# Inverse roots of the norms by ScalarE and small GpSimd products in place of GpSimd's power, and one more scan product on GpSimd

## The chip, the cores and the metric

The kernel runs on one core of one Trainium2 chip. Five engines of that core work side by side, each through its own list of instructions in a fixed order: PE (TensorE, matrix products), DVE (VectorE), ACT (ScalarE), POOL (GpSimd) and SP (SyncE, which here issues the transfers). An instruction starts when those before it on its engine have been taken up and the semaphores it waits for have been raised. The metric is the device time of one execution in microseconds (us).

## The reference

The input is 8 images of 64 channels and 128 x 128 pixels. Each goes through a small filter layer and then through a layer of this shape (cut to what matters here):

```python
def layernorm(x, w, b):
    mu = x.mean(-1, keepdims=True)
    var = ((x - mu) ** 2).mean(-1, keepdims=True)
    return (x - mu) * jax.lax.rsqrt(var + EPS) * w + b

def rmsnorm(x, w):
    return x * jax.lax.rsqrt((x * x).mean(-1, keepdims=True) + EPS) * w

def selective_scan(u, dt, A, Bm, Cm, D, z):
    dt = jax.nn.softplus(dt)
    dA = jnp.exp(jnp.einsum('bdl,dn->bldn', dt, A))
    dBu = jnp.einsum('bdl,bnl,bdl->bldn', dt, Bm, u)
    def comb(c1, c2):
        a1, h1 = c1
        a2, h2 = c2
        return (a1 * a2, a2 * h1 + h2)
    _, hs = jax.lax.associative_scan(comb, (dA, dBu), axis=1)
    y = jnp.einsum('bldn,bnl->bdl', hs, Cm) + D[None, :, None] * u
    return y * jax.nn.silu(z)

for i in range(DEPTH):                       # 2 blocks, each scanned forward and backward
    seq = bimamba_block(seq, ...)            # rmsnorm, projections, two selective_scans, residual
seq = rmsnorm(seq, normf_w)
...
xn = ln4d(x, norm2_w, norm2_b)               # and a feed-forward part with a GELU gate
```

Every norm needs the inverse square root of a mean plus EPS = 1e-5, one number per pixel. The scan runs over all 16,384 pixels of an image, for 128 channels with 16 states each.

## The kernel before

**The scan.** An image is cut into 16 chunks of T = 1024 pixels, and the four directions (two blocks, two ways each) make 64 chunks per image and 512 in all. A chunk has 16 steps u = 0 to 15, each a tile of 128 partitions x 1024 (channels times states). For a step, ACT computes the decay w = exp(a dt) into PSUM (`decay`, line 999), DVE runs the recurrence over 1024 pixels (`scan`, lines 1017 and 1019, one for each direction), and the result is multiplied by C (`product`, lines 1038 and 1041); PE then sums it into y (`collect`, line 1057). The other input of the scan, bu, is made by POOL for two steps at a time, a 128x2048 product with three buffers (`drive`, line 991). So a chunk has 8 drives on POOL and 16 scans on DVE.

**Who multiplies by C.** `on_pool(u)` decides it. It was: not for odd u, not for u = 4 and 12, not for a step just after a GELU, and for u = 8 only in chunks beside the front or the feed-forward part. A step on POOL has its scan written to hs, ACT keeps the last column as the state right after the scan, and POOL multiplies hs one step later (line 1038). A step on DVE has its scan written over w, DVE multiplies right after (line 1041), and ACT keeps the state after that (`keep`, line 1031). With this rule 2,832 of 8,192 products are on POOL.

**The norms.** A `Norm` (lines 400 to 421) squares elsewhere, has PE average the squares of 512 pixels into a 128x8 tile in PSUM (`means`), ACT add EPS and bring it to SBUF (`means_out`, line 411), POOL raise it to the power -0.5 (`root`, line 414), and PE spread the root over the channels (`spread`, line 420), for DVE to multiply with. There are 768: per image 16 x 3 in the front (the two norms that come before the scans, and the first block's), 16 in the mix stage, and 16 in each of the two second directions, where a block's result is normed for what follows.

**The order of the work.** Everything in the main part is put down with a time and a phase, `at(time, phase, fn)`; the list sorted by these two is the order in which the instructions of each engine stand, and nothing reorders them. Time is counted in scan steps; the phases of one step are FEED, SCAN, MID, PROD, DECAY, REST. Chunk i starts at 16 i, its drive k stands at 2k - 5, its products on POOL in FEED one step after their scan, its decay u two steps before its scan. Around the scans run other parts: the front of the next image (a piece every 24 steps, beside the second block), and of the image before the mix stage (every 13 steps, beside the first 12 chunks) and then the feed-forward part with its GELUs (every 24 steps, beside the rest of the first block and a little of the second). The core lines of a norm in a second direction:

```python
at(b + 12, FEED, lambda: n.means(mm_tile, self.sq))
at(b + 13, DECAY, n.means_out)
at(b + 14, REST, n.root)
at(b + 17, FEED, n.spread, mm_tile)
at(b + 18, DECAY, self.normed)
```

**Function tables.** ACT's Silu (line 895), Softplus (line 923), Gelu (line 763) and Exp (line 999) each need another table. The compiler puts a load ahead of the first instruction that needs another one than the one in place. Before, that is once ahead of each Silu, Softplus and Gelu group, and once ahead of the first decay after it.

Of the kernel before, what the change touches and what calls it, by code (L numbers as in the profile page):

```python
# [8 lines left out]
F32 = mybir.dt.float32  # L9
BF16 = mybir.dt.bfloat16  # L10
AF = mybir.ActivationFunctionType
ALU = mybir.AluOpType
# [3 lines left out]
P = 128  # L16
# [3 lines left out]
ROWS = 4  # L20
# [13 lines left out]
G = 4  # L34
U = G * G
PW = W + 2
FEED, SCAN, MID, PROD, DECAY, REST = range(6)

IMAGE = 4 * NT * U
# [16 lines left out]
def kernel(ctx: ExitStack, tc: tile.TileContext, a: dict, out: bass.AP):  # L56
# [6 lines left out]
    nc = tc.nc  # L63
# [8 lines left out]
    def const(shape, name, dt=F32):  # L72
        return wp.tile(shape, dt, tag=name, name=name)
# [3 lines left out]
    def dram(shape, name):  # L77
        return dramp.tile(shape, F32, tag=name, name=name + "_dram")


    def image(name):

        return dram([C, PW * PW + PW], name)

    def pixels(img):
        return img[:, 0 : PW * PW].rearrange("c (r w) -> c r w", w=PW)

    def clear(img):
        nc.sync.dma_start(
            img.rearrange("c (r w) -> c r w", w=PW),  # L90
            zero.rearrange("c (o w) -> c o w", o=1).to_broadcast([C, PW + 1, PW]),
        )

    x_img, xm_img, xn_img = image("x"), image("xm"), image("xn")
    dw_img = [image(f"dw{i}") for i in range(2)]
    zero = const([C, PW], "zero")
    nc.vector.memset(zero, 0.0)
# [11 lines left out]
    nc.vector.tensor_tensor(center, center, ident, ALU.add)  # L109
    eps = const([P, 1], "eps")  # L110
    nc.vector.memset(eps, EPS)
    neg_half = const([P, 2 * ROWS], "neg_half")
    nc.vector.memset(neg_half, -0.5)

    sel_y = const([P, 32, 1], "sel_y")
    nc.vector.tensor_reduce(sel_y, ident.rearrange("k (m n) -> k m n", n=G), AX.X, ALU.add)
# [44 lines left out]
    for h in range(2):  # L161
        nc.sync.dma_start(b1[h * 32 : (h + 1) * 32, :], row(a["L0_conv_b1"]))
        nc.sync.dma_start(w2v[64:65, 9 * h : 9 * h + 9], a["L0_conv_b2"].rearrange("(o k) -> o k", o=1))


    FRONT_W, MIX_W, FFN_W = 9 * 64 + P, 18 * P, 18 * P + 2 * C
    w_dram = [dram([P, n], f"w{i}") for i, n in enumerate((FRONT_W, MIX_W, FFN_W))]
# [190 lines left out]
    wk = ctx.enter_context(tc.tile_pool(name="wk", bufs=2))  # L358
# [19 lines left out]
    def tmp(name):  # L378
        return wk.tile([P, N], F32, tag="tmp", name=name, bufs=14)

    def window(img, name):

        return inp.tile([P, ROWS + 2, PW], F32, tag="win", name=name)

# [14 lines left out]
    class Norm:  # L399
# [7 lines left out]
                )  # L407

        def means_out(self):
            self.r = wk.tile([P, 2 * ROWS], F32, tag="r", name="r", bufs=4)  # L410
            nc.scalar.activation(self.r, self.mp[:, 0 : 2 * ROWS], AF.Identity, bias=eps)  # L411

        def root(self):
            nc.gpsimd.tensor_tensor(self.r, self.r, neg_half, ALU.pow)  # L414

        def spread(self, ps):
            self.rb = ps("rb")
# [15 lines left out]
    class Front:  # L433
        def __init__(self, b, c):
            self.b, self.c, self.p = b, c, b % 2
            self.n1, self.n2, self.n3 = Norm(), Norm(), Norm()
            self.t = {}
# [267 lines left out]
    class Ffn:  # L705
# [55 lines left out]
        def gelus(self):  # L761
            self.gt = tmp("gt")
            nc.scalar.activation(self.gt, self.rest[0], AF.Gelu)
            for h in range(2):
                nc.scalar.activation(self.ga[h], self.ga[h], AF.Gelu)

        def rest_times(self):
            nc.vector.tensor_tensor(self.gt, self.gt, self.rest[1], ALU.mult)
# [29 lines left out]
        def plan(self, a):  # L798
            early = 12 if self.alone else 0
            at(a - 4 - early, REST, self.load, 0)  # L800
            at(a - 3 - early, REST, self.load, 1)

            if self.alone:
                groups = ((0, 0, self.first_out, 2), (3, 2, None, 0), (6, 1, self.times, 9))
                gelus, out = 5, 12
            else:
                groups = ((0, 0, self.first_out, 5), (6, 2, None, 0), (14, 1, self.times, 19))
                gelus, out = GELU, 19
            for t, g, end, to in groups:
                for i in range(4):  # L810
                    at(a + t + (0 if self.alone else i), REST, self.conv, g, i)
                for h in range(2 if end else 0):
                    at(a + to, DECAY, end, h)
            at(a + gelus, REST, self.gelus)
            at(a + gelus + 1, DECAY, self.rest_times)
            at(a + out - 5, REST, self.load_x2)
            at(a + out, REST, self.project)
            at(a + out + 2, DECAY, self.add)
            at(a + out + 2, REST, self.store)

    def plan_ffn(b, a, step):
        at(a - 4, REST, load_weights, 2)
        for c in range(NCH):
            Ffn(b, c).plan(a + step * c)


    gelu_times = {IMAGE * b + FFN_AT + FFN_STEP * c + GELU for b in range(B - 1) for c in range(NCH)}
# [7 lines left out]
    class Chunk:  # L835


        def __init__(self, i):
            self.b, self.l, self.d, self.t, self.second = order[i]
            self.i, self.t0 = i, U * i  # L840
            self.first = i % NT == 0
            self.pairs = PAIRS[i % 2]
            r, last = self.t0 % IMAGE, self.b == B - 1
            self.beside_front = (
                FRONT_AT - FRONT_STEP <= r < FRONT_AT + NCH * FRONT_STEP + 16 and not last
            ) or self.t0 < FIRST_FRONT_AT + NCH * FRONT_STEP + 16
            self.beside_gelu = any(self.t0 - U <= t < self.t0 + 2 * U for t in gelu_times)
            self.prev = None
            self.bus, self.hss, self.ws = {}, {}, {}
            self.dup, self.dtp, self.bp, self.cp, self.yv = {}, {}, {}, {}, {}  # L850
            self.norm = Norm()
# [42 lines left out]
        def silu(self):  # L894
            nc.scalar.activation(self.xc, self.xc, AF.Silu)
            if self.second:
                nc.scalar.activation(self.gt, self.gt, AF.Silu)

        def store_gate(self):
            self.gt_d = sd.tile([DI, T], F32, tag="gate", name="gate_dram", bufs=4)  # L900
            nc.sync.dma_start(self.gt_d, self.gt)
            self.gt = {}
# [18 lines left out]
        def softplus(self):  # L921
            dt = self.dt
            nc.scalar.activation(dt, dt, AF.Softplus)

        def bc(self):
            self.bcp = mm_tile("bcp")
            for i, s in enumerate(halves):
                nc.tensor.matmul(
                    self.bcp[32 * i : 32 * i + 32, :], wbc[:, self.l, self.d, :], self.xc[:, s],
                    start=True, stop=True,  # L930
                )
# [45 lines left out]
        def on_pool(self, u):  # L977


            if u % 2 or u % 8 == 4 or self.t0 + u - 1 in gelu_times:  # L980
                return False
            return u != 8 or self.beside_front or self.beside_gelu

        def over_pair(self, what, k):
# [206 lines left out]
    for b in range(B):  # L1191
# [2 lines left out]
        plan_mix(b, a + (LAST_MIX_AT if last else MIX_AT), LAST_MIX_STEP if last else MIX_STEP)  # L1194
        plan_ffn(b, a + (LAST_FFN_AT if last else FFN_AT), LAST_FFN_STEP if last else FFN_STEP)
    with tc.manual_schedule():
        for key in sorted(steps):
            for fn, args in steps[key]:
                fn(*args)
# [29 lines left out]
```

## Time and profile before

The kernel's time is 30010.1 us (median of 3 runs, 30005.71 to 30014.66). The execution that was profiled took 29956.31 us and its span, from the first to the last instruction, is 29954.4 us.

| | busy us | share of the span | instructions |
|---|---|---|---|
| POOL | 27661.8 | 92% | 8732 |
| DVE | 27086.6 | 90% | 17258 |
| PE | 24257.7 | 81% | 96344 |
| ACT | 18533.8 | 62% | 28316 |

The scans run from about 580 us to 29337 us of the span; before them the weights are made ready and the first front runs, after them the last mix and feed-forward pieces. In a line of the profile, "L1038 POOL TENSOR_TENSOR hs<-hs,cp" is an instruction of line 1038 on POOL that writes the tile hs from hs and cp; then come shapes and count, the busy time in us and the mean duration of one in ns, and behind the last bar the idle time of that engine just before these instructions, with what ended it. A line of waits says who waited for whom, in us in total, how many times, and the longest.

### The profile page before, as it was taken

What the parts mean: (1) busy time and instruction counts of PE and PEld (TensorE: products, weight loads), DVE (VectorE), ACT (ScalarE), POOL (GpSimd) and SP (SyncE); (2) the same over time, 40 slices, a digit from 0 to 9 for tenths busy, and PEclk for the clock granted to TensorE, in tenths of its full rate; (3) what the DMA queues carried; (4) which work ended last, traced back from release to release, by engine and by line L of the source; (5) the groups of instructions that cost most, each with busy time, mean ns of one, the idle gap of its engine ahead of it and who ended that gap; (6) DMA issues with size and microseconds to landing.
All of it is one profiled execution on the core that took longest, in us unless ns stands there. A gap on an engine that the chain in (4) does not pass through costs nothing. (4 is left out here: it accounts for less than half of the span.)

```text
span 29954.4 us, 307972 instructions
## 1 busy us (share of the span) xinstructions
PE 24257.7 (81%) x96344; PEld 8093.1 (27%) x96344; DVE 27086.6 (90%) x17258; ACT 18533.8 (62%) x28316; POOL 27661.8 (92%) x8732
## 2 busy tenths in 40 slices
PE   7666888878888788887888788887888878888579
PEld 3211232223322233222322223222232223322123
DVE  3899999999999999999999999999999999999992
ACT  2566666666666666666666666666666666666661
POOL 3999999999999999999999999999999999999991
PEclk8777888988989888988899889898898988889789
DMA  4776676766777677776777767776677766777672
GB/s 100 210 241 214 221 235 230 237 213 223 237 231 237 213 225 237 232 232 210 233 232 238 225 214 232 232 237 223 215 236 232 240 214 222 235 234 234 214 240 75
DMA packets 2529698, 6617.29 MB, mean 221 GB/s; under 512 B 417862, under 2 KB 722262, under 8 KB 2525750
## 3 DMA queue, kind: packets, MB, share of 16 engines
q1 hardware_dynamic: 2528054, 6597.59, 68.4%
q8 instruction: 761, 12.47, 0.2%
q14 instruction: 883, 7.23, 0.1%
HBM read 5363.40 MB, written 1266.10 MB: 221 GB/s over the span
## 5 line engine op out<-in xcount | busy, mean ns | idle before, releaser
L991 POOL TENSOR_TENSOR bu<-dup,bp 128x2048 f32<-128x2048 f32 x4096 | 18578.8, 4539 | 557.7 <-DVE w L1019 421.4
L999 ACT ACTIVATE w<-dtp,a_neg 128x1024 f32<-128x1024 f32 x8192 | 9162.3, 1118 | 510.2 <-DVE hs L1017 313.9
L1038 POOL TENSOR_TENSOR hs<-hs,cp 128x1024 f32<-128x1024 f32 x2832 | 6685.3, 2361 | 197.9 <-ACT state L1031 133.3
L1041 DVE TENSOR_TENSOR hs<-w,cp 128x1024 f32<-128x1024 f32 x5360 | 6564.9, 1225 | 310.9 <-DMA cp<-bc_dram 77.6
L1017 DVE TENSOR_TENSOR_SCAN w<-w,state,bu 128x1024 f32<-128x1024 f32 x2677 | 6280.9, 2346 | 346.5 <-ACT w L999 345.9
L1019 DVE TENSOR_TENSOR_SCAN w<-w,state,bu 128x1024 f32<-128x1024 f32 x2683 | 6291.0, 2345 | 314.1 <-ACT w L999 313.5
L1057 PE MATMUL y<-hs,sel_y 128*32 128x512 f32 x32768 | 5183.3, 702 | 33.0 <-POOL hs L1038 32.6
L1031 ACT COPY state<-w 128x1 f32<-128x1 f32 x5360 | 837.4, 156 | 5040.0 <-DVE hs L1041 5004.5
L1017 DVE TENSOR_TENSOR_SCAN hs<-w,state,bu 128x1024 f32<-128x1024 f32 x1419 | 3321.3, 2341 | 86.4 <-ACT w L999 36.9
L1019 DVE TENSOR_TENSOR_SCAN hs<-w,state,bu 128x1024 f32<-128x1024 f32 x1413 | 3307.7, 2341 | 52.8 <-ACT w L999 34.7
L1050 PE MATMUL y<-xc,dskip 128*64 128x512 f32 x4096 | 1622.3, 860 | 2025.6 <-ACT yv L1074 1339.3
L869 PE MATMUL xp<-hn,wx 128*128 128x512 f32 x4096 | 2269.2, 682 | 485.3 <-ACT xc L875 339.8
L746 PE MATMUL fp<-fw,bgw 128*128 128x512 f32 (+1 forms) x6144 | 2353.9, 638 | 64.7 <-ACT ga L759 63.5
L1057 PEld LDWEIGHTS y<-hs,sel_y 128*32 128x32 f32 x32768 | 736.8, 116 | 3496.6 <-issue 2469.7
L1031 ACT COPY state<-hs 128x1 f32<-128x1 f32 x2832 | 540.2, 191 | 1829.2 <-DVE hs L1019 929.6
L414 POOL TENSOR_TENSOR r<-r,neg_half 128x8 f32<-128x8 f32 x768 | 1263.5, 1645 | 380.5 <-ACT r L411 323.9
L875 ACT ACTIVATE xc<-xp,cbias 128x512 f32<-128x512 f32 x1024 | 697.2, 681 | 1415.1 <-PE xp L869 1414.7
L910 PE MATMUL dp<-xc,wdt 128*128 128x512 f32 x2048 | 1228.5, 684 | 351.8 <-ACT dt L917 268.2
L752 PE MATMUL fp<-fw,bgw 64*128 64x512 f32 (+1 forms) x6144 | 1501.1, 608 | 0.0
L999 ACT ACT_TABLE_LOAD x1134 | 1454.9, 1283 | 20.1
L947 POOL TENSOR_TENSOR dt<-dt,xc 128x1024 f32<-128x1024 f32 x512 | 1212.8, 2369 | 246.5 <-DMA dt_dram<-dt 223.8
L510 PE MATMUL acc<-t,ident 128*128 128x512 f32 x2304 | 1361.3, 675 | 0.0
(184 smaller groups left out, 26903.7 us busy)
## 6 DMA issues: line engine op xcount, KB each, us to landing
bp<-bc_dram SPq DMA_DIRECT2D x4096, 256.0 KB, 4.0
dup<-du_dram SPq DMA_DIRECT2D x4096, 256.0 KB, 5.0
dtp<-dt_dram SPq DMA_DIRECT2D x4096, 256.0 KB, 5.0
cp<-bc_dram SPq DMA_DIRECT2D x4096, 256.0 KB, 5.0
hn<-hn_dram SPq DMA_DIRECT2D x1024, 256.5 KB, 4.8
dt_dram<-dt SPq DMA_DIRECT2D x512, 512.0 KB, 3.1
du_dram<-dt SPq DMA_DIRECT2D x512, 512.0 KB, 2.6
yf_dram<-yv SPq DMA_DIRECT2D x512, 256.0 KB, 4.4
```

What stands on the lines that cost most here:

```text
L746: nc.tensor.matmul(o, wpair[:, i, g, m], self.win[h][:, i : i + ROWS, 0:W], start=(i == 0), stop=False)
L752: nc.tensor.matmul(o, wlast[rows, i, g, m], self.win[h][rows, i : i + ROWS, lo : W + lo], start=False, stop=(i == 2),)
L869: nc.tensor.matmul(self.xp[h], wx[:, self.l, self.d, i, :], self.hn2[:, s.start + 2 * i : s.stop + 2 * i], start=(i == 0), stop=(i == 1),)
L991: nc.gpsimd.tensor_tensor(bu, self.dup[self.pairs[k][1]], self.over_pair("bp", k), ALU.mult)
L999: nc.scalar.activation(w, self.dtp[gp][:, i, :], AF.Exp, scale=a_neg[:, self.l, self.d, g, j : j + 1])
L1017: nc.vector.tensor_tensor_scan(to, w, bu, s0, ALU.mult, ALU.add)
L1019: nc.vector.tensor_tensor_scan(to[:, ::-1], w[:, ::-1], bu[:, ::-1], s0, ALU.mult, ALU.add)
L1031: nc.scalar.copy(self.column(u), h[:, T - 1 : T] if self.d == 0 else h[:, 0:1])
L1038: nc.gpsimd.tensor_tensor(hs, hs, c, ALU.mult)
L1041: nc.vector.tensor_tensor(hs, w, c, ALU.mult)
L1050: nc.tensor.matmul(self.y[C * h : C * h + C, :], dskip[:, self.l, self.d, C * gp : C * gp + C], self.xc[:, s], start=True, stop=False,)
L1057: nc.tensor.matmul(self.y[lo : lo + 32, :], sel_y, hs[:, i, s], start=False, stop=(k % 4 == 3))
```

## The change

In a norm, ACT now does four small activations on the 128x8 tile instead of one: r = ln(mean + EPS), v = mean + EPS, r = exp(-0.5 r), q = r squared. POOL does three small instructions instead of the power: q = q v, q = -0.5 q + 1.5, r = r q, which is one Newton step on the root. A function table that holds both Exp and Ln is asked for by name once at the start and right after each Silu, Softplus and Gelu group (the last image's GELUs excepted).

The second part is `on_pool`: step u = 4 is now on POOL in the chunks of a second direction beside the front, and in those chunks beside the feed-forward part whose steps 0 and 8 do not come just after a GELU. That is 175 of the 512 chunks (105 and 70), so 3,007 products are on POOL and 5,185 on DVE.

```diff
@@ -109,8 +111,6 @@
     eps = const([P, 1], "eps")
     nc.vector.memset(eps, EPS)
-    neg_half = const([P, 2 * ROWS], "neg_half")
-    nc.vector.memset(neg_half, -0.5)
 
@@ -162,6 +162,9 @@
+    def exp_and_ln():
+        nc.scalar.preload_act_table_set(EXP_AND_LN)
 
@@ -407,11 +410,18 @@
         def means_out(self):
-            self.r = wk.tile([P, 2 * ROWS], F32, tag="r", name="r", bufs=4)
-            nc.scalar.activation(self.r, self.mp[:, 0 : 2 * ROWS], AF.Identity, bias=eps)
+            mp, shape = self.mp[:, 0 : 2 * ROWS], [P, 2 * ROWS]
+            self.v, self.r, self.q = [wk.tile(shape, F32, tag=n, name=n, bufs=4) for n in ("rv", "r", "rq")]
+            nc.scalar.activation(self.r, mp, AF.Ln, bias=eps)
+            nc.scalar.activation(self.v, mp, AF.Identity, bias=eps)
+            nc.scalar.activation(self.r, self.r, AF.Exp, scale=-0.5)
+            nc.scalar.activation(self.q, self.r, AF.Square)
 
         def root(self):
-            nc.gpsimd.tensor_tensor(self.r, self.r, neg_half, ALU.pow)
+
+            nc.gpsimd.tensor_tensor(self.q, self.q, self.v, ALU.mult)
+            nc.gpsimd.tensor_scalar(self.q, self.q, -0.5, 1.5, ALU.mult, ALU.add)
+            nc.gpsimd.tensor_tensor(self.r, self.r, self.q, ALU.mult)
 
@@ -763,6 +773,8 @@
             for h in range(2):
                 nc.scalar.activation(self.ga[h], self.ga[h], AF.Gelu)
+            if not self.alone:
+                exp_and_ln()
 
@@ -845,6 +857,7 @@
             self.beside_gelu = any(self.t0 - U <= t < self.t0 + 2 * U for t in gelu_times)
+            self.skips = any(self.t0 + u - 1 in gelu_times for u in (0, 8))
@@ -895,6 +908,7 @@
             if self.second:
                 nc.scalar.activation(self.gt, self.gt, AF.Silu)
+            exp_and_ln()
 
@@ -921,6 +935,7 @@
             nc.scalar.activation(dt, dt, AF.Softplus)
+            exp_and_ln()
 
@@ -977,8 +992,10 @@
         def on_pool(self, u):
-            if u % 2 or u % 8 == 4 or self.t0 + u - 1 in gelu_times:
+            if u % 2 or u == 12 or self.t0 + u - 1 in gelu_times:
                 return False
+            if u == 4:
+                return self.beside_front and self.second or self.beside_gelu and not self.skips
             return u != 8 or self.beside_front or self.beside_gelu
 
@@ -1194,6 +1211,7 @@
     with tc.manual_schedule():
+        exp_and_ln()
         for key in sorted(steps):
```

`EXP_AND_LN` is the table's name, "natural_log_exp_and_others".

More of the change, by code (lines that the diff above doesn't have):

```diff
@@ L36 @@
 PW = W + 2
+EXP_AND_LN = "natural_log_exp_and_others"
 FEED, SCAN, MID, PROD, DECAY, REST = range(6)
```

## The prediction

> **What bounds the kernel now.** I read the page's groups of instructions first, then the waits, then the busy time of five steady stretches, and last the order of time around a table load. Groups (the last figures are the engine's idle time just before):
>
> ```profile
> L991 POOL TENSOR_TENSOR bu<-dup,bp 128x2048 f32<-128x2048 f32 x4096 | 18578.8, 4539 | 557.7 <-DVE w L1019 421.4
> L1038 POOL TENSOR_TENSOR hs<-hs,cp 128x1024 f32<-128x1024 f32 x2832 | 6685.3, 2361 | 197.9 <-ACT state L1031 133.3
> L1041 DVE TENSOR_TENSOR hs<-w,cp 128x1024 f32<-128x1024 f32 x5360 | 6564.9, 1225 | 310.9 <-DMA cp<-bc_dram 77.6
> L414 POOL TENSOR_TENSOR r<-r,neg_half 128x8 f32<-128x8 f32 x768 | 1263.5, 1645 | 380.5 <-ACT r L411 323.9
> L999 ACT ACT_TABLE_LOAD x1134 | 1454.9, 1283 | 20.1
> ```
>
> From all the groups, the rows that price the new small instructions:
>
> ```profile
> L667 POOL TENSOR_TENSOR x<-x,dwv 128x512 f32<-128x512 f32 x128 | 163.2, 1275 | 91.2 <-DVE dwv L664 91.2
> L487 POOL TENSOR_TENSOR lg<-lg,sp 128x72 f32<-128x72 f32 x256 | 84.0, 328 | 3.3 <-ACT sp L483 3.3
> L212 POOL MEMSET w2a<- 64x18 f32 x1 | 0.1, 106 | 0.0
> L411 ACT ACTIVATE r<-ms,eps 128x8 f32<-128x8 f32 x768 | 200.6, 261 | 54.7 <-PE ms L405 54.7
> L318 ACT ACTIVATE al<-al 128x16 f32<-128x16 f32 x4 | 0.9, 215 | 1.7 <-DMA al<-in_L_conv_A_log 1.7
> L476 DVE RECIPROCAL sm<-sm 128x8 f32<-128x8 f32 x128 | 26.0, 203 | 4.4
> ```
>
> The waits (us in total, times, longest):
>
> ```profile
> DVE w L1017 <- ACT w L999: 345.9, 302, 3.2
> DVE w L1019 <- ACT w L999: 313.5, 193, 3.2
> POOL r L414 <- ACT r L411: 323.9, 127, 19.1
> POOL r L414 <- ACT state L1031: 36.8, 14, 2.9
> POOL bu L991 <- POOL hs L1038: 1.5, 3, 0.7
> ```
>
> Five stretches of the third and the last image: beside the mix stage, beside the feed-forward part, beside the front in a first and in a second direction, and bare scans (span; PE, PEld, DVE, ACT, POOL busy):
>
> ```profile
> 7810.60:8362.60 552.00, 455.41 (x1715) 163.97 (x1717) 515.94 (x299) 342.49 (x515) 536.11 (x167) 0.91 0.72 235
> 8790.00:9458.50 668.50, 588.31 (x2409) 183.92 (x2410) 628.45 (x382) 442.87 (x652) 628.17 (x185) 0.94 0.73 240
> 9955.00:10471.90 516.90, 411.59 (x1682) 137.41 (x1678) 484.04 (x333) 329.93 (x526) 504.63 (x173) 0.86 0.64 209
> 10532.10:11295.90 763.80, 656.05 (x2881) 242.27 (x2880) 719.42 (x509) 504.94 (x810) 743.69 (x258) 0.90 0.71 228
> 27884.40:28387.10 502.70, 252.77 (x889) 54.90 (x888) 495.97 (x271) 315.26 (x453) 498.53 (x142) 0.71 0.63 213
> ```
>
> The reader is to see two engines that are nearly full, POOL a little fuller: 97% beside the mix stage (536.11 of 552.00) and beside the front (97.6% and 97.4%), with DVE at 93 to 94%; beside the feed-forward part both stand at 94%. DVE scans almost never wait for POOL; they wait for ACT's decays (731 us with the two smaller rows that write hs). POOL's lateness reaches DVE by a detour: PE stands in order behind products and roots of POOL, ACT behind PE, the decay behind that. So a microsecond off POOL is worth less than one, and I pass on 0.6 of POOL's change where POOL is at 97%.
>
> **The change part by part.** By the two built programs, PE's order and the main part of SP's are the same to the instruction; DVE loses 175 products, POOL gains them, ACT gains 2,304 small activations, and table loads go from 2,273 to 2,274. The one more is in the set-up, 1.3 us at most.
>
> *The root on POOL.* Removed: 1.645 us. Added: three 128x8 instructions, the second and third of which wait for the one before. From 128x512 (1275 ns) to 128x72 (328 ns) an element costs 2.15 ns, which puts a 128x8 one at 328 - 64 x 2.15 = 190 ns. Bounds: 106 ns (the memset) and 328 ns; I take 190, worked out from the rows of the same operation. POOL's instructions follow each other with an overlap of about 0.05 us (one started at 10899.98 for 2.38 us, the next at 10902.31); a dependent one can't. DVE's dependent reciprocal idles 4.4 us / 128 = 0.03 us; POOL behind its own product idled 1.5 / 3 = 0.5 us. I take 0.1 us for each of the two waits, nearer to DVE's row, because POOL's three cases may hold something else; bounds 0.03 and 0.5. So a root costs 3 x 0.19 + 2 x 0.1 = 0.77 us and saves 0.87 (between 3 x 0.106 + 0.06 = 0.38, saving 1.27, and 3 x 0.328 + 1.0 = 1.98, losing 0.34).
>
> *The product.* 175 x 2.361 = +413 us on POOL, 175 x 1.225 = -214 us on DVE. The name of the change promises one per chunk; it is 105 chunks beside the front in a second direction and 70 beside the feed-forward part.
>
> The Trainium skill speaks against this half: "GPSIMD Engine Reference", sections 3 and 4.1, holds GpSimd to be about 2x slower at two-input elementwise work (1.96x measured there) and sends it to VectorE. The rows here agree on the price, 2361 against 1225 ns. By the rule the move is a loss of 413 - 214 = 199 us; by the stretches, where two engines work side by side, it is a trade between them.
>
> *By stretch.* Counting the roots of line 414 in the time of each kind of chunk:
> - Beside the front, second direction: 105 chunks, 308 roots. POOL 105 x 2.361 - 308 x 0.87 = -20 us, DVE -129. POOL's part x 0.6 is -12; DVE's relief shortens POOL's waits for free bu buffers (421 + 116 us in all) and the detour, a quarter of it, -32. Together -44.
> - Beside the feed-forward part: 182 chunks, 126 roots, 70 products. POOL +165 - 110 = +56, DVE -86. At 94% both, half of DVE's counts, -43, and a quarter of POOL's, +14: -29.
> - The other 225 chunks: 307 roots, no product: POOL -267, x 0.6 = -160. The roots outside the scans (27) are not counted.
>
> *ACT.* Ln takes the place of Identity (0.26 us). Behind it: Identity, overlapped as the rows of ACT are (an instruction after a root's 0.25 us started 0.15 after it), +0.17; Exp and Square at line 318's 0.215, the last with a wait of 0.03: together +0.64 us for a root (0.5 to 0.9 with line 411's 0.26 for each and 0.1 for a wait), 492 us in all on an engine at 62%. Behind them in ACT's queue stand state copies and decays. Following each of the 768 from line 411 to where ACT next idles long enough, about 130 reach a scan that has no slack, for some 65 us; x 0.6 is +40. And POOL's root, next in its queue, starts later: 141 found POOL waiting for ACT already, 141 x 0.64 = 90, with some 20 us from those that had less slack than 0.64; 110 x 0.6 = +66. The PSUM tile of the means comes free 0.17 us later, which 28 waits of PE (47 us) show as 5 us: nothing.
>
> *Table loads.* They move, they don't grow. Before:
>
> ```profile
> 15018.24 1.06 ACT L895 ACTIVATE xc<-xc 128x1024 f32<-128x1024 f32 x1
> 15019.74 0.16 ACT L1031 COPY state<-w 128x1 f32<-128x1 f32 x1 [0.44 <-DVE hs L1041]
> 15019.92 1.28 ACT L999 ACT_TABLE_LOAD   x1
> 15021.21 1.12 ACT L999 ACTIVATE w<-dtp,a_neg 128x1024 f32<-128x1024 f32 x1
> ```
>
> Now the load stands right behind the Silu and takes part of the wait for DVE (0.44 us here). Over the 1,134 loads that idle time is 207 us. Scans that waited for a decay or a state copy right behind a load sum to 76 us; I take 40% of it, -30 (bounds 0 and -76).
>
> A page prices this otherwise: "ScalarE: Activation LUTs", section What ACT_TABLE_LOAD costs, adds a drain of about 1380 ns to the 1283, 2.66 us for a switch. The lines above leave no such gap ahead of the load or behind it. By the page up to twice as much could be hidden, at most -60; I keep to the rows.
>
> Sum: -44 - 29 - 160 + 40 + 66 - 30 = **-157 us**. The profiled execution took 29956 us, 54 below the median of 30010, so it would take 29799, and the median 30010 - 157 = 29853; I say **29850**.
>
> **Rivals.**
> - *All of it arrives.* Cheap roots and full passage: POOL -267 - 20, DVE half of 129 and 86, table loads -76, ACT's +106 as before: -267 - 20 - 65 - 43 - 76 + 106 = -365, so 29645. For it: POOL at 97%. Against it: its idle time comes from ACT and PE too.
> - *POOL was never the bound.* The loop of PE, ACT and DVE sets the pace and POOL just waits more. Then the 160 and the 12 are gone: -157 + 172 = +15, 30025. For it: scans wait for ACT and not for bu. It holds if DVE's idle time beside the mix stage (36 us of 552) stays.
> - *Slower: POOL's waits on itself.* If each of the two waits costs about the 0.5 us of the three cases, a root is 3 x 0.19 + 1.0 = 1.57 us and saves next to nothing: 0.8 us worse than my price over the 741 roots beside scans, x 0.6 = +356, so -157 + 356 = +199, 30209. It decides from -157 / (741 x 0.6) = 0.35 us above my price, a root of 1.12 us.
> - *Slower: ACT.* All 492 us land ahead of decays without slack: +492 in place of the 40, -157 + 452 = +295, 30305. For it: 731 us of scans waiting for decays. Against it: ACT idles 38% of the time, thousands of times ahead of a state copy.
>
> **How the numbers follow.** My case 0.45, all arrives 0.18, POOL not the bound 0.17, own waits 0.13, ACT 0.07. My case alone spans 29720 to 29945. The range goes from 29590 (below the first rival by the cheaper root, a saving of 1.27) to 30130, which leaves out most of the two slower cases. A change of 0.2%, 60 us, is about what can be told from none. Faster 0.63, same 0.17, slower 0.20.
>
> **What would show it.** A root on POOL of 0.6 to 0.95 us over three rows of 128x8, each under 0.3; POOL some 250 us less busy (27410), DVE some 210 (26870), ACT some 490 more (19020); the wait of POOL for ACT's part of the root 450 to 500 us in place of 361; scans' waits for decays not above 800; the stretch beside the mix stage shorter by 7 us in 552. Wrong would be three rows with idle time between them, POOL idle time growing by as much as the roots save, or many more waits of y for hs from line 1038, where u = 4 now makes five heavy slots in a row.

## The result, and the profile after

The changed kernel takes as long as the one before: 30007.26 us (median of 12 runs, 29978.85 to 30022.78) against 30003.22 us for the kernel before on the same chip (12 runs, 29969.07 to 30015.59). The ratio is 1.0002, with a 95% interval from 0.9994 to 1.0011. The forecast was 29850, that is 0.9947 of 30010. The profiled execution of the changed kernel took 30009.22 us, 2 above its median; that of the kernel before was 47 below its own (29956.31 against 30003.22), so a stretch of one profile is not to be held against the same stretch of the other to better than a few us in 500.

The page of the changed kernel, the busy times and the groups (total, mean ns | idle time just before, and what ended it):

```profile
span 30007.4 us, 311014 instructions
PE 24223.4 (81%) x96344; PEld 8073.1 (27%) x96344; DVE 26886.7 (90%) x17082; ACT 18903.1 (63%) x30621; POOL 27281.8 (91%) x10443
L1008 POOL TENSOR_TENSOR bu<-dup,bp 128x2048 f32<-128x2048 f32 x4096 | 18568.3, 4536 | 670.8 <-DVE w L1036 487.1
L1055 POOL TENSOR_TENSOR hs<-hs,cp 128x1024 f32<-128x1024 f32 x3007 | 7093.1, 2359 | 246.9 <-ACT state L1048 168.4
L1058 DVE TENSOR_TENSOR hs<-w,cp 128x1024 f32<-128x1024 f32 x5185 | 6350.3, 1225 | 316.4 <-DMA cp<-bc_dram 88.0
L422 POOL TENSOR_TENSOR rq<-rq,rv 128x8 f32<-128x8 f32 x768 | 160.4, 209 | 475.9 <-ACT rq L418 438.9 <-ACT state L1048 36.2
L424 POOL TENSOR_TENSOR r<-r,rq 128x8 f32<-128x8 f32 x768 | 156.1, 203 | 63.8
L423 POOL TENSOR_SCALAR rq<-rq 128x8 f32<-128x8 f32 x768 | 150.7, 196 | 67.2
L416 ACT ACTIVATE rv<-ms,eps 128x8 f32<-128x8 f32 x768 | 202.8, 264 | 0.0
L417 ACT ACTIVATE r<-r 128x8 f32<-128x8 f32 x768 | 162.8, 212 | 0.0
L418 ACT ACTIVATE rq<-r 128x8 f32<-128x8 f32 x768 | 160.4, 209 | 24.3
L167 ACT ACT_TABLE_LOAD x1137 | 1458.8, 1283 | 20.8 <-PEq L1236 0.7
```

The price of the root was right. Its three instructions take 209 + 196 + 203 ns, and the two waits between them 67.2 / 768 = 0.087 us and 63.8 / 768 = 0.083 us: 0.78 us against the 1.645 of the power. POOL is 380 us less busy, DVE 200 less, ACT 369 more, and the time is the same. POOL's 380 us stand, to a few us, in the idle time behind the last bars: 113 us more ahead of bu (557.7 before, 670.8 now), 49 more ahead of its hs products (197.9, now 246.9), 95 more ahead of the root (380.5, now 475.9), and 131 inside the root.

The waits of the changed kernel (total, times, longest):

```profile
POOL bu L1008 <- DVE w L1036: 487.1, 301, 3.4
POOL rq L422 <- ACT rq L418: 438.9, 120, 19.5
POOL bu L1008 <- DVE w L1034: 137.8, 160, 2.0
DVE w L1034 <- ACT w L1016: 375.1, 322, 3.2
DVE w L1036 <- ACT w L1016: 299.4, 184, 3.2
DVE w L1034 <- POOL bu L1008: 0.4, 1, 0.4
```

In 8,192 scans DVE found bu not ready twice, for 0.4 and 0.2 us (once before, for 0.7). POOL in turn waits 625 us for DVE to give back a bu buffer. It works ahead of DVE until its three buffers are full, and it did so before as well (421 + 116 us).

The stretches beside the mix stage, beside the feed-forward part, and beside the front in a first and in a second direction (span; PE, PEld, DVE, ACT, POOL busy; clock, DMA share, GB/s):

```profile
7828.00:8383.70 555.70, 461.52 (x1716) 165.72 (x1718) 516.44 (x299) 349.18 (x555) 522.03 (x193) 0.89 0.73 233
8814.60:9486.40 671.80, 593.64 (x2409) 185.96 (x2410) 623.76 (x378) 450.35 (x688) 624.98 (x213) 0.93 0.72 239
9981.60:10500.30 518.70, 415.43 (x1682) 138.49 (x1678) 484.40 (x333) 338.15 (x580) 487.97 (x209) 0.85 0.64 209
10556.20:11321.10 764.90, 659.36 (x2872) 243.23 (x2872) 704.23 (x495) 520.60 (x927) 734.80 (x349) 0.89 0.71 227
```

Beside the mix stage POOL is 14.1 us less busy and the stretch no shorter, so POOL idles 33.7 us of it in place of 15.9. DVE idled 36.1 us of the stretch before and idles 39.3 now. That DVE's idle time stays was the mark by which one would know the rival "POOL was never the bound". The 3.7 us by which the stretch is longer mean nothing: the same ten chunks stand in seven images, and in the kernel before they take 551.5 to 553.1 us in four of them and 560.3 to 560.5 in three (granted clock 0.90 to 0.91, and 0.89 to 0.90); in the changed kernel it is 555.7 to 555.8 in four and 559.1 to 559.4 in three (0.89). The means are 555.7 before and 557.3 after.

### The profile page after: what moved, and what is told of

It reads as the page before. It is cut to its first block, busy times and chain, and to the rows that moved or that the text cites. A ratio compares the mean times of both kernels' runs of the same rounds, so it can differ in the third digit from the quotient of the medians.

```text
span 30007.4 us, 311014 instructions
## 1 busy us (share of the span) xinstructions
PE 24223.4 (81%) x96344; PEld 8073.1 (27%) x96344; DVE 26886.7 (90%) x17082; ACT 18903.1 (63%) x30621; POOL 27281.8 (91%) x10443
## 5 line engine op out<-in xcount | busy, mean ns | idle before, releaser
L1008 POOL TENSOR_TENSOR bu<-dup,bp 128x2048 f32<-128x2048 f32 x4096 | 18568.3, 4536 | 670.8 <-DVE w L1036 487.1
L1055 POOL TENSOR_TENSOR hs<-hs,cp 128x1024 f32<-128x1024 f32 x3007 | 7093.1, 2359 | 246.9 <-ACT state L1048 168.4
L1058 DVE TENSOR_TENSOR hs<-w,cp 128x1024 f32<-128x1024 f32 x5185 | 6350.3, 1225 | 316.4 <-DMA cp<-bc_dram 88.0
L1036 DVE TENSOR_TENSOR_SCAN w<-w,state,bu 128x1024 f32<-128x1024 f32 x2634 | 6175.3, 2344 | 301.8 <-ACT w L1016 299.4
L1034 DVE TENSOR_TENSOR_SCAN w<-w,state,bu 128x1024 f32<-128x1024 f32 x2551 | 5984.1, 2346 | 375.9 <-ACT w L1016 375.1
L1034 DVE TENSOR_TENSOR_SCAN hs<-w,state,bu 128x1024 f32<-128x1024 f32 x1545 | 3616.3, 2341 | 132.8 <-ACT state L1048 64.4
L1036 DVE TENSOR_TENSOR_SCAN hs<-w,state,bu 128x1024 f32<-128x1024 f32 x1462 | 3422.1, 2341 | 144.9 <-ACT w L1016 92.1
L167 ACT ACT_TABLE_LOAD x1137 | 1458.8, 1283 | 20.8 <-PEq L1236 0.7
L756 PEld LDWEIGHTS fp<-fw,bgw 128*128 128x128 f32 (+1 forms) x6144 | 816.6, 176 | 1724.1 <-issue 1440.3
```

The costliest lines, as they stand in the source:

```text
L167: nc.scalar.preload_act_table_set(EXP_AND_LN)
L756: nc.tensor.matmul(o, wpair[:, i, g, m], self.win[h][:, i : i + ROWS, 0:W], start=(i == 0), stop=False)
L1008: nc.gpsimd.tensor_tensor(bu, self.dup[self.pairs[k][1]], self.over_pair("bp", k), ALU.mult)
L1034: nc.vector.tensor_tensor_scan(to, w, bu, s0, ALU.mult, ALU.add)
L1036: nc.vector.tensor_tensor_scan(to[:, ::-1], w[:, ::-1], bu[:, ::-1], s0, ALU.mult, ALU.add)
L1055: nc.gpsimd.tensor_tensor(hs, hs, c, ALU.mult)
```

## The experiments

The first theory after the result was that rival: PE, ACT and DVE pass work round in a fixed order, that sets the pace, and POOL only has to keep up. The theory on record, with POOL at 97% as the bound, had to hide its gain behind a loss of equal size, from the product, from ACT's new work or from the place of the table loads. Kernels are compared by their ratio to the kernel before on the same chip, with its 95% interval; the medians of the kernel before run from 29910 to 30003 from chip to chip.

**The two halves alone.** The roots without the moved product: `on_pool` as it was.

```diff
-            if u % 2 or u == 12 or self.t0 + u - 1 in gelu_times:
+            if u % 2 or u % 8 == 4 or self.t0 + u - 1 in gelu_times:
                 return False
-            if u == 4:
-                return self.beside_front and self.second or self.beside_gelu and not self.skips
```

> The new roots and the table loads without the moved product. Three theories of why 380 us less on POOL and 200 us less on DVE gave nothing. A, the order through PE: in most stretches the pace is set by a round trip of DVE's yv, PE's queue, ACT's xc and the decay, so relief on POOL and DVE turns into idle time and ACT's extra instructions fit beside it: 29980 to 30030. B, ACT ate it: relief passes at 0.6, and ACT's 490 us ahead of decays take it back; 668 us less on POOL give -400, ACT +330: about 29930. C, the move ate it: the roots alone bring 200, the moved product costs 200: about 29800.

The product without the roots: the kernel before with the new `on_pool` (and `skips`).

> The moved product alone, with the old power. A: DVE's 214 us less are idle time, and beside the front in a second direction POOL, at 97%, gets 2.36 us a chunk more where it idles 1.8, so a little slower there: 30020 to 30090. B: POOL +413 x 0.6 = +248, DVE -214 x 0.5 = -107: about 30140. C: about 30200.

The roots alone: 1.0005 (0.9995 to 1.0014). The product alone: 1.0051 (1.0036 to 1.0066), some 150 us. POOL is 777 us less busy in the first (26884.5), and nothing comes of it. In the second, POOL is full where the product was put: beside the front in a second direction it is busy 772.96 of 777.50 us, and PE's weight loads for y wait 601.6 us for its hs products (386.7 before).

```profile
10573.00:11350.50 777.50, 666.24 (x2881) 245.28 (x2880) 704.78 (x495) 503.48 (x810) 772.96 (x271) 0.88 0.70 224
PEld y L1060 <- POOL hs L1041: 601.6, 429, 5.5
```

The 105 chunks of that kind took 96 us more in this profile than in that of the kernel before, most of the 143 between the two profiles. So no loss from the product hides a gain of the roots: the roots have no gain to hide. What they do is make room on POOL for the product, which without them costs half a per cent.

**POOL's work, down and up.** The cleanest test of a bound is to take work off it and to put work on. One kernel leaves the power out, and ACT writes a constant 1 in its place (so the norms are not computed); one does a second power on constants behind each root.

```diff
-            nc.scalar.activation(self.r, self.mp[:, 0 : 2 * ROWS], AF.Identity, bias=eps)
+            nc.scalar.activation(self.r, self.mp[:, 0 : 2 * ROWS], AF.Identity, bias=one, scale=0.0)
         def root(self):
-            nc.gpsimd.tensor_tensor(self.r, self.r, neg_half, ALU.pow)
+            pass
```

> The kernel before with POOL's power left out; ACT's one instruction writes the constant 1 in its place, so the norms scale by 1 and the output is not the reference's. POOL loses 1263 us and every root reaches PE 1.6 us earlier. A: nearly nothing, 29930 to 30000, with POOL's idle time up by about 1200. B and C, relief passes at 0.6: about 29250.

```diff
         def root(self):
             nc.gpsimd.tensor_tensor(self.r, self.r, neg_half, ALU.pow)
+            nc.gpsimd.tensor_tensor(spare, half, neg_half, ALU.pow)
```

> The kernel before with a second power of 128x8 behind each root, on constants, for nobody: POOL +1263 us. A: it first fills POOL's idle time and costs only where that is used up; beside the front in a second direction 2.93 x 1.645 = 4.8 us a chunk against 1.8 idle, +3.0 x 105 = 315, in a first direction 2.7 against 1.75, +0.95 x 97 = 92: about 30400. B and C: +1263 x 0.6: about 30760.

Without the powers POOL is 1203 us less busy than before (27661.8, now 26458.5), and the ratio is 0.9996 (0.9987 to 1.0006): nothing, and at the end of the interval 39 us, 0.03 of what was taken away. The page and the waits of that kernel show where the time went:

```profile
PE 24297.8 (81%) x96344; PEld 8079.7 (27%) x96344; DVE 27084.1 (90%) x17259; ACT 18528.4 (62%) x28316; POOL 26458.5 (88%) x7964
...
POOL bu L993 <- DVE w L1021: 672.6, 357, 4.2
POOL bu L993 <- DVE w L1019: 451.5, 338, 4.3
POOL hs L1040 <- ACT state L1033: 312.1, 289, 10.9
```

The waits of POOL for a free bu buffer grow from 537 to 1124 us, those for the state copy ahead of its products from 133 to 312. The stretch beside the mix stage shows the same at an equal clock of 0.89: in this kernel (first row), and in the one with the moved product alone (second row), which changes nothing in these chunks and still has the power:

```profile
7801.30:8361.40 560.10, 466.58 (x1718) 167.37 (x1720) 516.06 (x299) 343.23 (x516) 514.04 (x153) 0.89 0.73 232
7836.50:8396.80 560.30, 467.26 (x1719) 167.66 (x1721) 516.09 (x299) 342.99 (x516) 535.84 (x167) 0.89 0.72 232
```

POOL is 21.8 us less busy and the stretch 0.2 us shorter. With the second power the ratio is 1.0165 (1.0150 to 1.0180), +496 us for 1201 us more of busy time on POOL (28862.5). The stretch beside the front in a second direction, the added instruction, and PE's waits for POOL:

```profile
10714.00:11519.00 805.00, 671.96 (x2873) 248.29 (x2872) 720.59 (x509) 505.40 (x810) 805.00 (x296) 0.88 0.68 218
L417 POOL TENSOR_TENSOR spare<-half,neg_half 128x8 f32<-128x8 f32 x768 | 1309.9, 1706 | 0.0
PE rb L423 <- POOL r L416: 461.9, 198, 5.0
PE y L1060 <- POOL hs L1041: 199.9, 157, 4.8
DVE hs L1020 <- POOL bu L994: 2.5, 2, 1.6
```

Here POOL is busy without a break, and its lateness reaches the scans through PE, as the prediction had it: PE's matmuls wait 462 us for roots (146 before) and 200 for hs (33 before), while DVE still waits 2.5 us for bu. Of the 488 us between the two profiles, 283 stand in those chunks and 124 beside the front in a first direction. So the detour is real, and it counts in one direction only. Up to the point where POOL is full, more work on it fills its idle time; beyond, it costs. The kernel before stands on the flat side of that point, but near it: the moved product alone, 388 us more on POOL, already cost 148.

**What does move the time.** Three kernels change the work of the other engines. ACT: three more small activations per norm on scratch tiles, as the change adds them. PE: one row of the last tap column left out of the feed-forward convolution. DVE: its product by C left out at u = 12.

```diff
+            nc.scalar.activation(s1, mp, AF.Identity, bias=eps)
             nc.scalar.activation(self.r, self.mp[:, 0 : 2 * ROWS], AF.Identity, bias=eps)
+            nc.scalar.activation(s1, s1, AF.Square, scale=-0.5)
+            nc.scalar.activation(s2, s1, AF.Square)
```

> The kernel before with three small activations more for every norm (one ahead of the root's Identity and two behind it, on scratch tiles for nobody), 0.6 us of ACT for a root, 480 us in all, as much as the change adds to it; POOL and DVE as before. If ACT's extra work is what took the gain: 150 to 300 us slower. If the pace is set by the order through PE and ACT fits the work into its idle time: within 60 us.

```diff
-            for i in ((), (), (0,), (1, 2))[part]:
+            for i in ((), (), (0,), (2,))[part]:
```

> The kernel before with one of the three rows of the last tap column left out of the feed-forward part's products (2,048 of 12,288 instructions of that part, about 500 us of PE, of which 438 stand beside scans and 62 in the last image's tail; the output is not the reference's). Theory A1, PE's queue sets the pace beside the feed-forward part, 182 chunks that lose 2.4 us of PE each: half or more arrives, with the tail -62: 270 to 400 us faster. A2, PE only follows (waits for yv and for xc), and what counts are fixed waits of DVE for ACT: the tail's 62 and little more, 60 to 120 us faster.

```diff
-            to = hs if self.on_pool(u) else w
+            to = hs if self.on_pool(u) or u == 12 else w
...
+            if u == 12:
+                return
```

> The kernel before without DVE's product for step 12 in every chunk (512 x 1.225 = 627 us of DVE; the scan writes hs and the state is kept right after it; the output is not the reference's). If DVE is the full engine, all of it arrives: 600 us faster. Theory A (A1 and A2 alike): where scans wait for ACT the relief is idle time; only stretches in which DVE is at 98% give it back: 50 to 250 us faster.

| | change in busy time | ratio | in us |
|---|---|---|---|
| POOL less (no power) | -1203 | 0.9996 (0.9987 to 1.0006) | -6 |
| POOL more (second power) | +1201 | 1.0165 (1.0150 to 1.0180) | +496 |
| ACT more (three activations) | +333 | 1.0010 (1.0001 to 1.0019) | +29 |
| PE less (a row of taps) | -357 | 0.9923 (0.9908 to 0.9938) | -220 |
| DVE less (512 products) | -592 | 0.9952 (0.9937 to 0.9967) | -141 |

The microseconds are the differences of the medians of one chip. PE, the engine with a busy share of 81%, gives back most per microsecond: 220 us for 357, or for 440 if only line 752 is counted, where the matmuls are left out (1501.1 us busy, now 1061.0). The rest of PE is 83 us more busy, at a mean granted clock of 0.876 in place of 0.881. Of the 289 us between the two profiles, 192 come in the 182 chunks beside the feed-forward part and 54 in the tail, where no scan runs. DVE gives back a quarter, POOL, at 97% in three of the five stretches, nothing. ACT's added work costs a tenth of what it takes.

**The round trip.** If no engine's sum sets the pace, an order must. The timeline of the kernel before, in the stretch beside the feed-forward part, shows it (start, duration, engine and line; in brackets the idle time and what ended it):

```profile
9249.44 0.68 DVE L1072 TENSOR_TENSOR yv<-y,gate 128x512 f32<-128x512 f32 x1
...
9250.18 1.98 PE L1050 MATMUL y<-xc,dskip 128*64 128x512 f32 x4 [3.91 <-DVE yv L1072]
...
9265.11 2.33 DVE L1019 TENSOR_TENSOR_SCAN w<-w,state,bu 128x1024 f32<-128x1024 f32 x1
...
9268.59 1.99 PE L752 MATMUL fp<-fw,bgw 64*128 64x512 f32 x8
...
9270.51 1.98 PE L869 MATMUL xp<-hn,wx 128*128 128x512 f32 x4
...
9272.53 0.69 ACT L875 ACTIVATE xc<-xp,cbias 128x512 f32<-128x512 f32 x1 [3.04 <-PE xp L869]
9273.12 0.15 ACT L1031 COPY state<-w 128x1 f32<-128x1 f32 x1
9273.16 1.13 ACT L999 ACTIVATE w<-dtp,a_neg 128x1024 f32<-128x1024 f32 x1
...
9274.32 2.36 DVE L1019 TENSOR_TENSOR_SCAN w<-w,state,bu 128x1024 f32<-128x1024 f32 x1 [2.40 <-ACT w L999]
```

PE waits 3.91 us for DVE's yv. From 9250.18 to 9272.5 its queue then runs without a gap, through the sums of y, the projection and the feed-forward matmuls down to xp. ACT stands at `conv_out` (line 875) and waits 3.04 us for xp, with a state copy and a decay behind it; and DVE, at the end, waits 2.40 us for that decay. Over the stretch no engine is full (PE 88%, DVE and POOL 94%), though PE is for these 22 us, and all of them wait in turn. DVE's yv, PE's queue, ACT's xc and the decay make one round, and POOL is in no part of it here. Over the whole kernel ACT waits 1414.7 us for xp; how often the round closes as in these lines was not counted.

To test this, two edits shift the order and take no work away. The first puts the matmuls for xp at the end of the step before, ahead of the next step's; the second puts `rest_times`, a DVE product that waits for the GELU, one step later.

```diff
-                at(b + 7 + h, FEED, self.conv, h)
+                at(b + 6 + h, REST, self.conv, h)
```

> The kernel before with the chunk's first convolution (PE xp) put into REST one step earlier, ahead of the other parts' products of that step; its ACT part stays. A1: ACT reaches xc earlier (it waits 1415 us for xp) and the decays behind it too: 80 to 250 us faster. A2: the same direction, under 100 us. If the transfer of hn is late instead (PE waits 99 us for it), the gain is gone or turns into a loss of up to 60 us.

```diff
-            at(a + gelus + 1, DECAY, self.rest_times)
+            at(a + gelus + (1 if self.alone else 2), DECAY, self.rest_times)
```

> The kernel before with the feed-forward part's product gt (line 768) one step later on DVE, except in the last image's tail, so that DVE does a scan while ACT does the GELU (DVE waits 528 us for gt in 123 places, about 2.1 us in each of the 112 beside scans). A2: nearly all of it arrives, 150 to 230 us faster. A1: PE's burst behind it decides, and DVE waits for decays instead: under 80 us faster.

The first gives 0.9986 (0.9976 to 0.9995). By the profiles it gains 72 us beside the feed-forward part and 57 in the chunks with neither front nor feed-forward work, and loses 48 beside the front in a second direction. ACT's wait for xp falls from 1415 to 635 us and DVE's for the decays from 659 to 442, and yet only 47 us come of it: the total of a wait is not its price. The second gives 0.9999 (0.9990 to 1.0009): DVE's waits for the GELU fall from 528 to 356 us, and the time does not. Then both at once, the first left as it was beside the front in a second direction; on the kernel before, and on the changed one:

```diff
+            now = max(b + 6, 0) % IMAGE
+            early = not (48 * U <= now < FRONT_AT + NCH * FRONT_STEP + 16) or self.b == B - 1
...
-                at(b + 7 + h, FEED, self.conv, h)
+                at(b + 6 + h if early else b + 7 + h, REST if early else FEED, self.conv, h)
```

> The kernel before with the first convolution a step earlier except in the time beside the front in a second direction, where it had cost 48 us, and with gt a step later: the round trip through PE is shorter and no engine does less. If the gains of the two edits stand side by side (56 beside the mix stage and the rest, 72 + 43 beside the feed-forward part): 130 to 190 us faster. If both took the same wait away: 60 to 130 us.

> The change with the same two edits of the order. If POOL and DVE come closer to being the bound once the round trip is shorter, the change is now worth something: 40 to 150 us faster than the edits on the kernel before. If the round trip still decides: the same as them, within 30 us.

On the kernel before: 0.9955 (0.9941 to 0.9969), 29787.63 against 29922.67 us, with every engine doing the same instructions. It is faster than both kernels of this case. Its page and waits:

```profile
PE 24172.7 (81%) x96344; PEld 8075.7 (27%) x96344; DVE 27098.4 (91%) x17258; ACT 18536.6 (62%) x28316; POOL 27655.5 (93%) x8732
...
ACT xc L875 <- PE xp L869: 779.0, 447, 16.7
POOL bu L991 <- DVE w L1019: 244.3, 185, 2.9
DVE w L1017 <- ACT w L999: 282.2, 262, 3.2
DVE w L1019 <- ACT w L999: 194.7, 210, 1.6
```

ACT's wait for xp is down from 1415 to 779 us, DVE's for decays from 659 to 477, and POOL's for free buffers with them. On the changed kernel the same edits give 0.9993 (0.9985 to 1.0002), although ACT's wait for xp falls to 903 there too. I had thought that the cheap roots would be worth something once the round was shorter. The opposite holds: on this order the change costs 0.4% (0.9955 against 0.9993, intervals apart).

So the order alone moves the time; that it does so through this round is argued from the waits and not shown by itself. The sizes were not foretold well either: the moved product alone cost 148 us where the round theory said 10 to 80 (30020 to 30090), the row of taps gave 220 between the two forecasts (270 to 400, 60 to 120), and the first edit of the order 47 where 80 to 250 stood under A1.

One thing came along that no run here separates, PE's granted clock. Its median is 0.884 with both edits and 0.880 in the kernel before and with the edits on the changed kernel. Among 33 runs of the kernel before on one chip, 0.001 more of clock goes with about 9 us less; by that, an estimate, 0.004 would be some 36 of the 135 us that the edits win, and of the 112 that the change takes away again. Whether the clock is a cause there or follows from how PE is kept busy stays open.

**Where the change costs on the better order.** One suspect was the place of the table loads, now ahead of a state copy. The kernel before with only the loads moved; the changed kernel with the loads back, right ahead of the decay one step later; that with the better order; and that without the moved product.

```diff
+BEFORE_DECAY = PROD + 0.5
...
-            exp_and_ln()
...
+            at(b + SILU + 1, BEFORE_DECAY, exp_and_ln)
+            at(b + SOFTPLUS + 1, BEFORE_DECAY, exp_and_ln)
```

> The kernel before with the table of Exp and Ln asked for right behind each Silu, Softplus and Gelu group, as the change does it, and nothing else: as many loads, each now ahead of a state copy that DVE or POOL may wait for. If the place of the loads is what the roots alone lose beside the feed-forward part (+37 us there, though neither POOL's relief nor ACT's extra work costs anything by itself): 30 to 120 us slower. As the prediction had it (the load takes part of a wait): 30 us faster.

> The change with the loads back in their old place, behind the state copy and right ahead of the decay. If their place costs: 40 to 120 us faster than the change, so that it stands 30 to 100 us below the kernel before. If it doesn't: the same as the change, within 40 us of the kernel before.

> The two edits of the order, the change, and the loads in their old place. The edits alone took 135 us off, the edits with the change 23. If the place of the loads is what the change costs there: 100 us or more come back, 29780 to 29820 on this chip's scale. If it is the moved product: it stays near 29890.

> The same without the moved product: the two edits of the order, the new roots, loads in their old place. If the place of the loads is the cost: as the edits alone, 29770 to 29800. If the moved product is: also there, and 100 us below the run that has it. If the new roots themselves cost: near 29890.

The loads moved alone: 0.9999 (0.9990 to 1.0008). Moved back: 1.0006 (0.9997 to 1.0015), and on the better order 0.9993 (0.9985 to 1.0002), just as with the loads ahead of the state copy. So the place of the loads is worth nothing that can be told from zero either way, and that suspicion fell. In the kernel before, the copy right behind the Silu waited 0.44 us, and the next one 0.93:

```profile
15023.26 0.16 ACT L1031 COPY state<-w 128x1 f32<-128x1 f32 x1 [0.93 <-DVE hs L1041]
```

The timeline of the changed kernel shows the same place, where the load was meant to gain:

```profile
15039.96 1.28 ACT L167 ACT_TABLE_LOAD   x1
15041.25 0.16 ACT L1048 COPY state<-w 128x1 f32<-128x1 f32 x1
15041.45 1.12 ACT L1016 ACTIVATE w<-dtp,a_neg 128x1024 f32<-128x1024 f32 x1
15043.91 0.16 ACT L1048 COPY state<-w 128x1 f32<-128x1 f32 x1 [1.34 <-DVE hs L1058]
```

The load does take up the wait ahead of the state copy; the next copy waits 1.34 us for DVE, so that what was saved comes back there. The Trainium skill, "ScalarE: Activation LUTs", section What ACT_TABLE_LOAD costs, would add a drain of about 1380 ns per switch. Neither this timeline nor the 20.8 us of idle time ahead of 1,137 loads has room for it.

Without the moved product the better order gives 0.9976 (0.9968 to 0.9985). So of the 0.38% that the change costs there, the product is about 0.17% and the roots 0.21%; each pair of intervals touches, so the shares are rough. The three activations per norm cost 0.10% on the order before and may be the roots' part; whether they are was not settled.

## Why the prediction was wrong

**The step that failed** is the last sentence on what bounds the kernel: "a microsecond off POOL is worth less than one, and I pass on 0.6 of POOL's change where POOL is at 97%". The detour through PE that it rests on exists, as the second power shows. But it was taken for a slope that runs both ways. Downwards the share is 0 (1203 us off, ratio 0.9996, at most 0.03), and with it go the 160 us of the 225 other chunks, more than the whole sum of 157, and the 12 us beside the front. The prediction quoted the waits that tell it: POOL idles 421 + 116 us for free bu buffers, and DVE "almost never" waits for POOL. An engine that waits for its consumer to give buffers back is ahead of it. I read these waits as time to be won by relieving DVE, not as the proof that POOL was not late. The step takes the +66 for POOL's later roots with it, which had the same 0.6; without the three terms the sum is -51, still outside the measured -18 to +33. Without the -30 of the table loads, which did not show either, it is -21. So DVE's relief, -32 and -43, was too large as well: the half of it that was to arrive beside the feed-forward part was a quarter where DVE's work was measured alone, and the product that brings the relief costs time by itself.

**The rival that came true** is "POOL was never the bound", at 30025: that is 15 us over 30010, and the measured difference is 4 (-18 to +33 by the interval). It was given 0.17. Its mechanism is the one that the runs show; that its number came within 11 us is in part luck, since it kept the +66, the -30 for the table loads and the -75 for DVE's relief, none of which the runs can tell from nothing.

**Point by point.**
- The root on POOL, 0.77 us: 0.78 measured, with instructions of 0.20 us and waits of 0.085. The rival with waits of 0.5 us falls.
- POOL 250 us less busy: 380. The 250 had the waits inside the root in it, 131 us, which do not count as busy. DVE 210 less: 200. ACT 490 more: 369, since the added rows were counted at 0.64 us for a root and overlap to less.
- The product, -44 and -29 us for the two kinds of chunk: nothing measurable, since the kernel with the roots alone is at 1.0005 and with both at 1.0002. DVE's relief was counted at a quarter to a half; a quarter is what leaving 512 products out gives (141 us of 592). What it may win here POOL's extra work seems to take back; the two were not measured apart. The Trainium skill's rule against the move ("GPSIMD Engine Reference", sections 3 and 4.1) is nearer to the runs than the trade that I made of it: +0.51% by itself, about +0.17% on the better order, and free only where the roots had made room.
- ACT, +40 and +66: the waits came about as predicted (475 us for ACT's part of the root, 450 to 500 said; 810 us of scans for decays, just over the 800 that was named as the most). Their price did not: three more activations per norm cost 29 us (3 to 57) and the roots as a whole +0.05% (-0.05 to +0.14). POOL's later roots cost little because POOL has time to wait.
- Table loads, -30: nothing (0.9999); the interval of 0.9990 to 1.0008 just reaches -30.
- The stretch beside the mix stage, 7 us shorter: 3.7 longer in the image shown, 1.6 in the mean of seven, with POOL's idle time up by 17.8 in the image shown. A difference of 7 could not have been told there, where the kernel before is itself 8 us apart from image to image. "POOL idle time growing by as much as the roots save" was named as the mark of being wrong, and it is what happened. Many more waits of y for hs, another such mark, did not come: PE's matmuls and weight loads together wait 450 us for them, 419 before.

## What to carry to other kernels

A busy share of 97% does not make an engine the bound: ask who waits for whom. If it waits for free buffers and its consumer never waits for it, work taken off it was worth nothing here, though work put on it soon cost. Before pricing a change, find the round of waits in the timeline (here yv, PE's queue, xc, decay, scan) and price only what lies in it. Moving two groups of instructions in the order was worth more here (0.45%) than 1203 us off the fullest engine (0.04%, not told from none). And look at a stretch in every image before reading a few us out of one: the same work took 552 or 560.

## What the runs showed of the hardware that I had not expected

An instruction of POOL that needs the result of the one before starts 0.085 us after it ends (0.083 and 0.087 in the two places of the root), a sixth of the 0.5 us that three cases of the kernel before suggested. And a mean duration on POOL is no pace: with a second power behind each root the power's mean is 1706 ns in place of 1645 and that of the 128x2048 product 4582 in place of 4539, but the records overlap by more, as the starts in that kernel's timeline show:

```profile
10952.01 1.71 POOL L416 TENSOR_TENSOR r<-r,neg_half 128x8 f32<-128x8 f32 x1
10953.61 1.71 POOL L417 TENSOR_TENSOR spare<-half,neg_half 128x8 f32<-128x8 f32 x1
10955.22 4.59 POOL L994 TENSOR_TENSOR bu<-dup,bp 128x2048 f32<-128x2048 f32 x1
```

From start to start a power takes 1.60 us here, as in the kernel before (one starts at 10937.35, the next instruction at 10938.95), though the rows say 1706 and 1645 ns. So 768 powers, 1263 us in their row, are 1229 us of POOL's pace, nearer to the 1203 by which POOL was less busy without them.

The kernel before ran 0.3% apart on different chips (medians from 29910 to 30003), more than several of the effects above, which therefore show only beside it on the same chip.
